# Filter loop of a hybrid layer: chunk buffers laid apart, banks read back one by one, loop transfers in parts of 128 KB behind the first half of a quarter's products

## The chip, the cores and the metric

One core of a Trainium2 chip. The metric is the device time of one execution in microseconds (us). The kernel before was run three times: 1398.19, 1403.44 and 1407.6 us, a median of 1403.44 us. One more execution was profiled.

## The reference, cut to what matters

The program takes `x`, 8 sequences of 1024 tokens with 128 channels, through two residual layers. Layer 0 is attention over normalised heads; layer 1 is a two-directional state-space block and then a spectral filter. The change lies wholly in the spectral filter and in the hand-over to it, so only that is shown:

```python
def _compute_spectral(u, sigma, phi, Mpp, Mpm):
    U_plus, U_minus = _stu_conv(phi, u, PADDED_SL)     # FFT convolution of u with 16 filters
    s = sigma ** SIGMA_POW
    out = jnp.einsum('btkd,k,kde->bte', U_plus, s, Mpp)
    return out + jnp.einsum('btkd,k,kde->bte', U_minus, s, Mpm)
...
t = t + _L1_ffn_ref(_ln_t(t), ...)                     # spectral filter + three-tap regression
```

The kernel does the convolution in the frequency domain: it transforms the normalised tokens to 128 frequencies, forms for each frequency a matrix (128 by 128, for several phases) out of the filters' spectra and the mixing matrices, multiplies, and transforms back.

## The kernel before, in words

Three stages of the program matter here. Engines run the instructions of each stage in the order in which they are written; in the first two groups below this holds for TensorE, VectorE, ScalarE and GpSimd (`IN_ORDER`), while the DMA issues of SyncE (SP) are placed by a planner.

**The preparing stage** (pools `f_1`, `f_2`, about 998 to 1069 us in the profile). A loop over sequences `b` = 2 to 8. `transform(b)` turns the tokens (`cpt`, L561), makes their spectra on TensorE (`pf`, L571), combines them on VectorE and GpSimd (`sd` L582, `sp` L586 and L589) and stores 1 MB of spectra to DRAM (`ud`, L592). `taps_of(b - 1, k)` makes the three-tap regression (`pu`, L601), `add_taps` adds it to the residual `X` (L611), and `store_residual` writes 512 KB of `X` to DRAM (`xa`, L614). In between, `turned(n)`, for b = 2 to 5, reads a quarter of the mixing bank, 512 KB (`md`, L1568), turns it on TensorE (`mdt`, L1573), copies it (`me`, L1574) and stores it (L1577). Only after the fourth bank are all four read back, in four transfers of 512 KB, into the tile `mst` (L1580), which the filter loop multiplies with. `reload(u)` (L1320), the last read-back of a residual, stands in the stage before it.

**The filter loop** (pools `g_2`, `g_3`). 16 chunks of 8 frequencies, software pipelined: iteration `c` makes the matrices of chunk `c + 1` and applies those of chunk `c`, in four quarters. A quarter is two calls of `matrices` (TensorE `pg`, L1644, four PSUM tiles each, copied out to `gs` by ScalarE, L1657, and VectorE, L1655, in turn) and two calls of `apply` (TensorE `py`, L1678), then `gather` (L1693 to L1699). The input spectra of a chunk come in two transfers of 256 KB (`u`, L1664), for which GpSimd then makes a second, rotated copy (L1667, L1668). Every second quarter stores 256 KB of sums (`yd`, L1701); `fetch` reads a part of an earlier chunk's sums back (`early_yt`, L1709). `gs` and `u` are double-buffered tiles of the pool `g_2`. That pool takes the memory which the residuals `X` held, so its first writers wait until the last `xa` store has read them.

**The last chunk and the inverse transform.** In the last iteration no matrices are made; instead 3 MB of residuals are asked for in two transfers (`load_residuals`, L1712). After it the sums are read back (L1753), transformed (`pz`, L1769), added to the residuals (L1776) and written out (L1779).

Of the kernel before, what the change touches and what calls it, by code (L numbers as in the profile page):

```python
# [14 lines left out]
P = 128  # L15
B = 8
# [29 lines left out]
def fast_kernel(ctx: ExitStack, tc: tile.TileContext, a: dict, out: bass.AP, bad: bass.AP):  # L46
# [883 lines left out]
    with ExitStack() as s:  # L930
# [611 lines left out]
        reload(u)  # L1542
# [10 lines left out]
    with ExitStack() as s:  # L1553
        mp = s.enter_context(tc.tile_pool(name="c_m", bufs=1, side="right"))
        mst = mp.tile([P, 32, C], F32, tag="mst", name="mst")
        early_yt = mp.tile([P, 2, 4, 4, C], F32, name="early_yt")

        with ExitStack() as s2:
            p1 = s2.enter_context(tc.tile_pool(name="f_1", bufs=1))
            p2 = s2.enter_context(tc.tile_pool(name="f_2", bufs=2))  # L1560
            ps_f = s2.enter_context(tc.tile_pool(name="f_ps_f", bufs=2, space=PSUM))
# [3 lines left out]
            def turned(n, pool, tag, size):  # L1565

                t = p2.tile([P, 8, C], F32, tag="md", name=f"md{n}")
                nc.sync.dma_start(t, md.rearrange("d r k e -> d (r k) e")[:, n * 8 : n * 8 + 8, :])  # L1568
                to = p2.tile([P, 8, C], F32, tag="me", name=f"me{n}")
                for at in range(0, 8, size):  # L1570
                    pt = pool.tile([P, size, C], F32, tag=tag, name=f"mdt{n}_{at}")
                    for i in range(size):
                        nc.tensor.transpose(pt[:, i, :], t[:, at + i, :], ident)  # L1573
                    nc.vector.tensor_copy(  # L1574
                        to[:, at : at + size].rearrange("p k d -> p (k d)"), pt.rearrange("p k d -> p (k d)")
                    )
                nc.sync.dma_start(me[:, n * 8 : n * 8 + 8, :], to)  # L1577
                if n == 3:
                    for g in range(4):
                        nc.sync.dma_start(  # L1580
                            mst[g * 32 : (g + 1) * 32],
                            me[g * 32 : (g + 1) * 32].rearrange("n k d -> k n d"),
                        )
# [23 lines left out]
            s2.enter_context(tc.manual_schedule(engines=IN_ORDER))  # L1607
            uts = {}
            for _ in scaled(3, *third, p2):
                pass  # L1610
            for b in range(2, B + 1):
                if b + 2 < B:
                    norms[b + 2] = normalize(p2, b + 2)
                if b < B:
                    transform(b)
                if 3 < b + 1 < B:
                    for _ in normalized(b + 1, p2, *norms.pop(b + 1), wide=p2):
                        pass
                if b > 2:
                    taps_of(b - 1, 0)  # L1620
                if 2 <= b <= 5:
                    turned(b - 2, *((ps_o, "o", 4) if b == 2 else (ps_t, "t", 8)))
                if b > 2:
                    taps_of(b - 1, 1)
                    store_residual(b - 1)
        middle.close()
        middle.close()

        with ExitStack() as s2:
            p2 = s2.enter_context(tc.tile_pool(name="g_2", bufs=2))  # L1630
            p3 = s2.enter_context(tc.tile_pool(name="g_3", bufs=3))
            ps_g = s2.enter_context(tc.tile_pool(name="g_ps_g", bufs=8, space=PSUM))

            turn = 0

            def matrices(c, n, gs):

                nonlocal turn
                pts = [ps_g.tile([P, 4, P], F32, tag="g", name=f"pg{c}_{n}_{g}") for g in range(4)]
                cols = slice(c * FC, (c + 1) * FC)  # L1640
                for e in range(4):
                    for g in range(4):
                        rows = slice(g * 32, (g + 1) * 32)
                        nc.tensor.matmul(  # L1644
                            pts[g][:, e, :],
                            lhsT=mst[rows, n * 4 + e, :],
                            rhs=taps[rows, cols].rearrange("p f q m i -> p (f q m i)"),
                            start=True,
                            stop=True,
                        )  # L1650
                for g, pt in enumerate(pts):
                    to = gs[:, :, n * 16 + g * 4 : n * 16 + g * 4 + 4]
                    frm = pt.rearrange("p e n -> p n e")
                    if turn % 2:
                        nc.vector.tensor_copy(to, frm)  # L1655
                    else:
                        nc.scalar.copy(to, frm)  # L1657
                    turn += 1

            def loaded_spectra(c):  # L1660

                u = p2.tile([P, 2, NB, B, 2, 4 * FC], F32, tag="u", name=f"u{c}")
                for k in range(NB):
                    nc.sync.dma_start(  # L1664
                        u[:, 0, k].rearrange("p b i f -> p b (i f)"), ud[c][:, :, k].rearrange("p b i q f -> p b (i q f)")
                    )
                nc.gpsimd.tensor_scalar(u[:, 1, :, :, 0, :], u[:, 0, :, :, 1, :], -1.0, None, ALU.mult)  # L1667
                nc.gpsimd.tensor_copy(u[:, 1, :, :, 1, :], u[:, 0, :, :, 0, :])  # L1668
                return u
# [50 lines left out]
            for c in range(-1, chunks):  # L1720
# [21 lines left out]
                if c > 0:  # L1742
                    fetch(c - 1)
# [847 lines left out]
```

## Time and profile before

| quantity | us |
|---|---|
| median of three runs | 1403.44 |
| profiled execution, its own time | 1403.45 |
| its span, first to last instruction | 1401.6 |
| preparing stage | about 998 to 1069 |
| first matrices to first application | 1069.2 to 1088.4 |
| filter loop, first application to that of the last chunk | 1088.4 to 1340.8 |
| last chunk | 1340.8 to 1356.4 |
| inverse transform and output | 1356.4 to 1401.6 |

All times below that are places on the axis are counted from the first instruction of the profiled execution. PE is TensorE's matmul, PEld its weight load, DVE VectorE, ACT ScalarE, POOL GpSimd, SPq the DMA issues of SyncE. A row of the windows view gives, for a stretch A:B, the length, then the busy time of PE, PEld, DVE, ACT and POOL with the number of instructions in brackets, then the share of full clock granted to TensorE (PEclk), the mean busy share of the 16 DMA engines and the rate in GB/s. A row of the waits view reads: who waited, for whom, the total in us, how often, and the longest. A row of the timeline gives start and length of a run of like instructions, and in brackets the idle time before it and what ended it; "issue" stands for a wait that the profile cannot put down to any engine or transfer.

### The profile page before, as it was taken

To read this page: it belongs to the slowest core of one execution; us is meant where nothing else is said; L and a number is where in the kernel's file an instruction comes from. 1 tells how busy PE (TensorE), PEld (TensorE's weight loads), DVE (VectorE), ACT (ScalarE), POOL (GpSimd) and SP (SyncE) were. 2 spreads that over 40 slices of the span, in tenths; PEclk is the share of its full clock that TensorE was granted. 3 is DMA by queue.
4 is the path that set the end of the run, shared out by engine and by line. 5 is a ranking of instruction groups with operands and counts; after the bars stand their busy time and mean duration, and the time that the engine had idled before them with its cause. 6 is when DMAs were issued, how large, how long until landed. Compare 5 with 4: busy or idle time off the path is not lost. (4 is left out here: it accounts for less than half of the span.)

```text
span 1401.6 us, 47569 instructions
## 1 busy us (share of the span) xinstructions
PE 1330.1 (95%) x20926; PEld 844.7 (60%) x20926; DVE 1103.4 (79%) x2145; ACT 922.8 (66%) x1428; POOL 536.0 (38%) x510
## 2 busy tenths in 40 slices
PE   7999999999999999999999999998898999999967
PEld 4333333333333666666666666667797988888964
DVE  5789888788778688988889898999564777777745
ACT  5666666766756888888878888876353555555520
POOL 3412986876910343434343343444673011111100
PEclk9999999999999999999999999999999999999979
DMA  7100111111101434444444343431668132222357
GB/s 172 55 2 2 38 39 39 53 39 39 31 1 42 96 78 93 108 94 113 94 108 94 92 95 88 114 83 48 197 208 198 46 78 73 77 69 70 83 171 294
DMA packets 139391, 123.24 MB, mean 88 GB/s; under 512 B 44808, under 2 KB 118152, under 8 KB 135080
## 3 DMA queue, kind: packets, MB, share of 16 engines
q1 hardware_dynamic: 137048, 115.93, 32.0%
q8 instruction: 166, 2.72, 0.8%
q10 hardware_dynamic: 2128, 4.19, 0.8%
q14 instruction: 49, 0.40, 0.1%
HBM read 78.15 MB, written 34.08 MB: 80 GB/s over the span
## 5 line engine op out<-in xcount | busy, mean ns | idle before, releaser
L809 ACT ACTIVATE pr<-pt 128x1024 f32<-128x1024 f32 x256 | 248.2, 1022 | 105.0 <-PE pt L804 103.9
L1657 ACT COPY gs<-pg 128x512 f32<-128x512 f32 x256 | 133.1, 603 | 75.6 <-PE pg L1644 58.4
L1655 DVE COPY gs<-pg 128x512 f32<-128x512 f32 x256 | 159.1, 685 | 26.0 <-PE pg L1644 18.9
L834 DVE TENSOR_TENSOR two<-pr,pr 128x1024 f32<-128x1024 f32 x128 | 164.8, 1328 | 15.2 <-ACT pr L809 15.2
L804 PE MATMUL pt<-q,k 32*128 32x512 f32 x1024 | 162.5, 651 | 6.1 <-ACT pr L809 4.1
L1644 PE MATMUL pg<-taps,mst 32*128 32x128 f32 x4096 | 150.1, 283 | 11.9 <-issue 5.8
L1644 PEld LDWEIGHTS pg<-taps,mst 32*128 32x128 f32 x4096 | 135.0, 189 | 27.2 <-issue 19.3
L825 PE MATMUL po<-pr,v 128*32 128x512 f32 x1024 | 140.6, 610 | 0.0
L1678 PE MATMUL py<-gs,u 128*32 128x128 f32 (+1 forms) x4096 | 130.9, 281 | 3.4 <-issue 3.4
L1030 POOL TENSOR_TENSOR ec<-ec,ct 128x2048 f32<-128x2048 f32 x16 | 83.6, 5224 | 112.3 <-ACT ct L1110 57.1
L1072 DVE SCALAR_TENSOR_TENSOR xs<-xp,cw,xs 128x1024 f32<-128x1024 f32 x96 | 122.5, 1283 | 2.2 <-issue 0.2
L1678 PEld LDWEIGHTS py<-gs,u 128*32 128x32 f32 (+1 forms) x4096 | 114.8, 141 | 10.9 <-issue 3.6
L1094 PE MATMUL pb<-bxt,wbc 128*128 128x512 f32 x256 | 114.0, 597 | 3.6 <-ACT zs L1085 3.6
L1667 POOL TENSOR_SCALAR u<-u 128x512 f32<-128x512 f32 x16 | 24.0, 1499 | 237.5 <-DMA u<-ud 138.3
L804 PEld LDWEIGHTS pt<-q,k 32*128 32x128 f32 x1024 | 49.5, 185 | 88.9 <-ACT pr L809 27.1
L1193 DVE SCALAR_TENSOR_TENSOR state<-state,dec,pst 128x64 f32<-128x64 f32 x448 | 87.3, 275 | 1.1
L1302 POOL TENSOR_TENSOR rms<-rms_v,mhalf 128x8 f32<-128x8 f32 x16 | 26.5, 1659 | 157.0 <-DVE rms_v L1300 157.0
L1094 PEld LDWEIGHTS pb<-bxt,wbc 128*128 128x128 f32 x256 | 47.1, 189 | 60.3 <-issue 55.0
L825 PEld LDWEIGHTS po<-pr,v 128*32 128x32 f32 x1024 | 27.8, 110 | 89.7 <-issue 86.4
L1016 POOL TENSOR_TENSOR lm<-cs,lm 128x2048 f32<-128x2048 f32 x16 | 57.9, 3620 | 57.7 <-DVE xs L1072 22.6
L845 PE MATMUL pd<-two,ones 128*32 128x512 f32 x512 | 74.1, 618 | 2.3 <-DVE two L834 2.1
L1272 PEld LDWEIGHTS spo<-wo,y 128*128 128x128 f32 x512 | 62.1, 191 | 13.1 <-issue 8.9
(310 smaller groups left out, 2784.5 us busy)
## 6 DMA issues: line engine op xcount, KB each, us to landing
lm<-cd SPq DMA_DIRECT2D x32, 512.0 KB
ec<-cd SPq DMA_DIRECT2D x32, 512.0 KB
ud<-sp SPq DMA_DIRECT2D x8, 1024.0 KB
u<-ud SPq DMA_DIRECT2D x32, 256.0 KB
yd<-sums SPq DMA_DIRECT2D x32, 256.0 KB
moved<-state SPq DMA_DIRECT2D x48, 128.0 KB
room<-yd SPq DMA_DIRECT2D x6, 1024.0 KB
X<-in_x SPq DMA_DIRECT2D x8, 512.0 KB
```

The source lines that it names most:

```text
L804: nc.tensor.matmul(pt[:, i, :], lhsT=k[rows, j * P : (j + 1) * P], rhs=q[rows, cols], start=True, stop=True)
L809: nc.scalar.activation(pr[:, 2 * g : 2 * g + 2, :].rearrange("p i t -> p (i t)"), pt.rearrange("p i t -> p (i t)"), AF.Exp, scale=SCALE,)
L825: nc.tensor.matmul(po[rows, :], lhsT=vs[b][:, j, rows], rhs=pr[:, h, :], start=(j == 0), stop=(j == NT - 1))
L834: nc.vector.tensor_tensor(two, sums["pr"][:, 2 * g : 2 * g + 2, :], pr[:, 2 * g : 2 * g + 2, :], ALU.add)
L1030: t = nc.gpsimd.tensor_tensor(u.ec, u.ec, u.ct.unsqueeze(1).to_broadcast([P, NH, NT, L]), ALU.mult)
L1072: u.convolved = nc.vector.scalar_tensor_tensor(acc, xp[:, at : at + T], cw[u.d][:, n, i : i + 1], acc, ALU.mult, ALU.add)
L1094: nc.tensor.matmul(u.pb[:, i * 512 : (i + 1) * 512], lhsT=wbc[u.d][:, k, :], rhs=xt[:, at : at + 512], start=(k == 0), stop=(k == KC - 1),)
L1193: nc.vector.scalar_tensor_tensor(u.state[:, k, h, :], u.state[:, k - 1, h, :], u.dec[:, c, h, j : j + 1], u.pst[c][:, j, h, :], ALU.mult, ...
L1644: nc.tensor.matmul(pts[g][:, e, :], lhsT=mst[rows, n * 4 + e, :], rhs=taps[rows, cols].rearrange("p f q m i -> p (f q m i)"), start=True, ...
L1655: nc.vector.tensor_copy(to, frm)
L1657: nc.scalar.copy(to, frm)
L1678: nc.tensor.matmul(py[t * 32 : t * 32 + 32 - 16 * m, q // 2, :], lhsT=u[:, i, m:, :, :, q * FC + f].rearrange("p k b i -> p (k b i)"), rhs ...
```

## The change

Six edits.

1. `gs` and `u` of even chunks live in a pool `c_g`, opened before the preparing stage on the other side of the memory; those of odd chunks in a pool `g_g` opened with the loop. Chunk 0's buffers thus no longer lie over the residuals. `early_yt` moves to a pool of its own that opens with the loop. The wide temporaries of the preparing stage get their own pool `f_x`.
2. Banks are loaded ahead (`load_bank`): three before the loop over `b`, the fourth when the first has been turned. `turned` moves from b = 2 to 5 to b = 3 to 6. `reload` of the last residual moves behind the first bank load.
3. Each bank is read back by itself (`spread(n)`, at the head of b = 4 to 7): sixteen transfers of 128 KB instead of four of 512 KB.
4. The first two of the eight `matrices` calls of chunk 0 are made inside the preparing stage, at b = 8, one between the last two tap blocks and one after them (`double_banks`, using the PSUM banks of the spectra). Chunk 0's spectra are asked for at the end of that stage.
5. In the loop every `u` comes in four parts of 128 KB with their own pair of GpSimd copies, every `yd` store in two halves, and the residuals in six transfers of 512 KB. Each of these, and `fetch`, is made to wait (`behind`) for the last matmul of the first of the two `apply` calls in a quarter; only the first half of each store follows the `gather` instead.
6. SP's DMA issues are in written order too, in both stages (`ALL_IN_ORDER`).

The numbers of matmuls, of evictions and of bytes are the same.

```diff
-        early_yt = mp.tile([P, 2, 4, 4, C], F32, name="early_yt")
+        first_gs = s.enter_context(tc.tile_pool(name="c_g", bufs=1, side="right"))
...
+        def load_part(u, c, part, other=None):
+            k, h = divmod(part, 2)
+            bs = slice(4 * h, 4 * h + 4)
+            t = nc.sync.dma_start(
+                u[:, 0, k, bs].rearrange("p b i f -> p b (i f)"), ud[c][:, bs, k].rearrange("p b i q f -> p b (i q f)")
+            )
+            if other:
+                behind(t, other)
+            nc.gpsimd.tensor_scalar(u[:, 1, k, bs, 0, :], u[:, 0, k, bs, 1, :], -1.0, None, ALU.mult)
+            nc.gpsimd.tensor_copy(u[:, 1, k, bs, 1, :], u[:, 0, k, bs, 0, :])
...
+            def spread(n):
+                for g in range(4):
+                    nc.sync.dma_start(
+                        mst[g * 32 + n * 8 : g * 32 + n * 8 + 8],
+                        me[g * 32 : (g + 1) * 32, n * 8 : n * 8 + 8].rearrange("n k d -> k n d"),
                     )
-                nc.sync.dma_start(me[:, n * 8 : n * 8 + 8, :], to)
-                if n == 3:
-                    for g in range(4):
-                        nc.sync.dma_start(
-                            mst[g * 32 : (g + 1) * 32],
-                            me[g * 32 : (g + 1) * 32].rearrange("n k d -> k n d"),
-                        )
...
-            s2.enter_context(tc.manual_schedule(engines=IN_ORDER))
+            s2.enter_context(tc.manual_schedule(engines=ALL_IN_ORDER))
+            for n in range(3):
+                load_bank(n)
+                if n == 0:
+                    reload(units[-1])
...
+            planned = {(B, 1): 1, (B, 2): 1}
             for b in range(2, B + 1):
+                if 4 <= b <= 7:
+                    spread(b - 4)
...
                 if b > 2:
                     taps_of(b - 1, 0)
-                if 2 <= b <= 5:
-                    turned(b - 2, *((ps_o, "o", 4) if b == 2 else (ps_t, "t", 8)))
+                ahead(b, 1)
+                if 3 <= b <= 6:
+                    turned(b - 3)
...
+            us = {0: loaded_spectra(0, first_gs)}
+            for part in range(4):
+                load_part(us[0], 0, part)
...
+            def amid_products(c, n, made):
+                if n == 0 and c > 0:
+                    store(c - 1, 1, 1, late_sums.pop((c - 1, 1)), made)
+                if n == 2:
+                    store(c, 0, 1, late_sums.pop((c, 0)), made)
+                if c + 1 < chunks:
+                    for part in ((0,), (1, 2), (3,), ())[n]:
+                        load_part(us[c + 1], c + 1, part, made)
+                if c > 0 and n >= 2:
+                    fetch(c - 1, n - 2, made)
+                if c + 1 == chunks:
+                    for _ in range(2 if n < 2 else 1):
+                        waiting.pop(0)(made)
...
-                        apply(c, half, turn, gs[c], us[c], py)
+                        made = apply(c, half, turn, gs[c], us[c], py)
+                        amid_products(c, n, made)
                         apply(c, half, turn + 2, gs[c], us[c], py)
                         gather(c, half, turn, py)
+                        behind_products(c, n)
```

## The prediction

> **What bounds the kernel now.** I read the page's first part, then a table of windows cut at the stage boundaries, then the waits and the timeline inside the bad windows.
>
> ```profile
> PE 1330.1 (95%) x20926; PEld 844.7 (60%) x20926; DVE 1103.4 (79%) x2145; ACT 922.8 (66%) x1428; POOL 536.0 (38%) x510
> ```
>
> TensorE is busy for 95% of the span, so a gain must come from places where it idles or runs below its clock. The windows view finds them (columns: PE, PEld, DVE, ACT, POOL, clock, DMA share, GB/s).
>
> ```profile
> 1003.00:1008.00 5.00, 0.00 (x1) 0.03 (x1) 1.39 (x3) 1.49 (x3) 5.00 (x11) 0.91 0.99 292
> 1008.00:1015.00 7.00, 7.00 (x27) 6.38 (x28) 3.48 (x18) 0.35 (x1) 3.37 (x7) 0.58 1.04 346
> 1015.00:1053.00 38.00, 38.00 (x293) 36.61 (x293) 24.31 (x62) 20.63 (x48) 27.31 (x53) 1.00 0.62 209
> 1069.00:1076.00 7.00, 2.07 (x64) 1.88 (x64) 0.25 (x2) 0.19 (x1) 0.00 (x0) 0.96 0.66 235
> 1076.00:1082.00 6.00, 5.55 (x93) 5.56 (x97) 4.99 (x8) 4.01 (x8) 0.89 (x1) 0.50 0.94 178
> 1088.40:1340.80 252.40, 246.52 (x7554) 224.71 (x7553) 184.84 (x413) 138.08 (x296) 28.83 (x28) 1.00 0.27 71
> 1340.80:1356.40 15.60, 12.11 (x321) 11.56 (x320) 4.34 (x15) 2.19 (x8) 0.00 (x0) 0.78 0.70 243
> ```
>
> Two stalls of 5 us, at 1003 and at 1071, are each followed by 6 to 7 us at about half clock; the loop has 6 us of idle matmul time; the last chunk idles and loses clock too. The waits between 995 and 1090 us name the first two stalls:
>
> ```profile
> ACT gs L1657 <- DMA xa<-X: 16.5, 1, 16.5
> PE mdt L1573 <- DMA md<-md: 5.1, 1, 5.1
> PE pg L1644 <- ACT gs L1657: 5.2, 1, 5.2
> ```
>
> The first turning waits for the load of bank 0; later the PSUM tiles fill because the first copies into `gs` wait for the last residual store. In the loop the timeline shows a quarter without and one with a stall:
>
> ```profile
> 1111.11 2.26 PE L1644 MATMUL pg<-taps,mst 32*128 32x128 f32 x64
> 1113.29 2.01 PE L1678 MATMUL py<-gs,u 128*32 128x128 f32 x64
> 1115.24 2.25 PE L1644 MATMUL pg<-taps,mst 32*128 32x128 f32 x64
> ...
> 1121.15 0.52 SPq L1664 DMA_DIRECT2D u<-ud  x1
> 1121.52 2.01 PE L1678 MATMUL py<-gs,u 128*32 128x128 f32 x64
> 1123.46 1.16 PE L1644 MATMUL pg<-taps,mst 32*128 32x128 f32 x29
> 1124.87 1.38 PE L1644 MATMUL pg<-taps,mst 32*128 32x128 f32 x35 [0.25 <-issue]
> ```
>
> A free quarter takes 1115.24 - 1111.11 = 4.13 us. The stalled one breaks in the middle of `pg` with no engine or transfer to wait for, 2 to 4 us after a `u` load. The last chunk has the same, longer:
>
> ```profile
> PE py L1678 <- issue: 3.4, 1, 3.4
> ```
>
> [...] queue q8, kind "instruction", 166 packets and 2.72 MB, 16 KB each. [...] the DMA records of the loop do show one about every 4.1 us. In free quarters around 1113 it starts as `py` starts (1113.32 against 1113.29) and takes 0.9 to 1.5 us; at 1122 it starts 0.73 us late, amid `u` packets. I read "issue" as a late fetch. [...] between 1338.73 and 1347.19 no fetch is recorded while residual packets fill the engines. [...]
>
> **The change part by part.** (a) Banks ahead. Bank 0 is now wanted at b = 3 and its load is issued where it was, at 1001, so the 5.1 us wait goes. What is late next: the second `transform` needs the PSUM tile that ScalarE copies out until 1004.5, so `cpt` of b = 3 starts at 1004.5 instead of 1009.7, a 1.6 us idle remaining. An undisturbed b with a turning takes 10.56 us (`cpt` at 1022.36 and 1032.92). Before, b = 7 began at 1053.17; after, 1004.5 + 4 x 10.56 = 1046.8. That includes the fourth turning, about 1 us, moved into b = 6. Gain 6.4 us: the wait, plus the half-clock tail.
>
> The DMAs moved on SP's ordered queue: bank 0's load now has the `xa` store of b = 1 and `reload` behind it; `reload` waits for its own store (2.3 us before) with two bank loads behind it, both wanted ten us and more later; each `spread` waits for the `me` store before it, and the next `ud` store stands behind that. Does `mst` come in time? The fourth bank is copied near 1045; its store stands behind the `ud` of b = 6, ready near 1047.6 (6.7 us behind its `pf`, as before). At 346 GB/s (window 1008 to 1015) that 1 MB, the 512 KB of `me` and the 512 KB of `xa` take some 6 us, and the last spread, 512 KB at the 180 GB/s seen while `mst` was read (1055 to 1061), 3 more: landing near 1057. From the head of b = 7 to the end of the taps it took 1069.22 - 1053.17 = 16.05 us; the first early `matrices` stands one tap block (2.7 us) before its end, at 1046.8 + 13.4 = 1060.2. So 3 us of slack; if everything runs at 180 GB/s, about 3 us are lost, and clock with them. I take 0.
>
> (b) Chunk 0 ahead, own memory. From the end of the taps to the first application it took 1088.4 - 1069.2 = 19.2 us. Now the first `gs` copies wait for nothing. Eight calls lie behind the taps (six of chunk 0, two of chunk 1), paced by VectorE: two copies of 0.685 us per call, 1.4 us, so 11.2 us, and 1.2 us at the start because the PSUM banks of the second early call must be emptied: 12.4. The early call inside the taps adds 1.05 us. Gain 19.2 - 13.4 = 5.8 us. The last two `xa` stores and chunk 0's `u` (1.5 MB, 4.5 us at 346 GB/s, behind `ud` of b = 7) and the GpSimd copies of `u`, with nothing queued behind them there, are hidden under these 12 us; with that cover gone they cost 0 to 3 us. (a) and (b): 12 us, 8 to 14.
>
> (c) Loop. 58 quarters lie between the `pg` runs at 1090.38 and 1338.64: 248.3 us against 58 x 4.12 = 239.0, so 9.3 us of stalls. A trigger halfway through `py` comes 1 us after the fetch began; packets follow an issue by 1 us, and 128 KB is half of the 1.5 us that a 256 KB load takes, so one or two parts lie between 2.0 and 3.7 us after `py`'s start, the next fetch at 4.1. The half store behind `gather` still meets the fetch, with half its bytes. But fetches late in the loop begin with `pg` (1309.95 against 1309.90), where parts now fall. Gain 0 to 9.3; a loss up to 3 if more parts mean more meetings; I take 7. The bill elsewhere: 8 GpSimd copies of 128 x 128 instead of 2 of 128 x 512 (1.50 and 0.61 us) per chunk. Bounds: 2.1 us if only elements count, 8.4 if a copy costs the same; I take 3, hidden either way beside a 16.5 us chunk. SP waits behind TensorE: the last part is issued 11.4 us into a chunk, and is wanted at 18.6; landing (3 us) and two copies leave about 3 us.
>
> (d) Last chunk. Four `apply` pairs of 1.95 us are 7.8; it takes 15.6. The same 3 MB in 512 KB pieces still fill 8 us at 390 GB/s, so a fetch can still be late, by one or two pieces instead of by 2 MB. Gain 0 to 7.8; I take 4. The extra store and its issue cost 0.3 us before the final read-back, whose 7.4 us stall stays.
>
> Sum: 12.2 + 7 + 4 - 0.3 = 22.9 us. The profiled execution took 1403.45 us (span 1401.6), the median is 1403.44, so the same sum serves: 1380.5.
>
> **The rivals.** One: only the hand-over gains, because the fetch drifts into the parts and the last chunk stays as it is: 1403.4 - 12 = 1391. For it: the phase late in the loop, and the unchanged bytes. Against it: two thirds of the quarters run free even now, and the long breaks follow a `u` load. Two: everything is recovered, 14 + 9.3 + 6 = 29: 1374. For it: free quarters are exactly periodic. Three, slower: SP's ordered queue makes the parts of `u` late. If the wake-up, landing and GpSimd copies of part 3 take over 7.2 us, TensorE stands at each chunk's first `apply`; at 3 us beyond that, 15 chunks cost 45 us: 1403.4 - 12 + 45 = 1436; it becomes slower overall from about 1 us per chunk. Against it: a `u` load before was followed by its GpSimd copy 5 us after the second issue (1121.15 to 1126.11), 256 KB and twice the copy. Four: `mst` late and clock lost again, hand-over gains 5, the loop nothing: 1398. That the transfers do not move is ruled out by the built order: SP's issues do wait on TensorE.
>
> **How the numbers follow.** Forecast (1376 to 1389) 0.56, rival two (1369 to 1376) 0.18, rival one (1389 to 1395) 0.13, rival four 0.06, rival three 0.07. The range 1369 to 1395 leaves out 0.13 by the cases and a little for a hand-over better than counted. One per cent, 14 us, is about what a measurement of this kernel can tell from no change: below 1389.4 is faster (0.75), up to 1417 the same (0.18), above it slower (0.07).
>
> **What would show it.** `cpt` of b = 7 near 1047; no wait of `mdt` for `md` nor of `gs` for `xa`; the first application near 1076 with full clock before it; quarters of 4.1 us with "issue" gaps under 3 us in all; the last chunk near 11 us. Wrong if `pg` waits for `mst`, if `py` waits for GpSimd's copies, or if the "issue" gaps are as many as before at other places.

## The result, and the profile after

The changed kernel takes 1416.64 us, the median of six runs (1416.10 to 1419.77), against 1401.54 us for the kernel before beside it: a ratio of 1.0109 with a 95% interval of 1.0083 to 1.0135. It is slower by about 1%; 1380.5 was forecast. The profiled execution took 1416.49 us with a span of 1414.7, so 13.0 us more than the one before (1403.45 and 1401.6). Cut at the same events in both traces, the 13.1 us of the spans are made up like this:

| stretch | before, us | after, us | difference | forecast |
|---|---|---|---|---|
| start to `cpt` of b = 0 | 962.24 | 963.13 | +0.9 | 0 |
| `cpt` of b = 0 to `cpt` of b = 7 | 90.93 | 84.60 | -6.3 | -6.4 |
| `cpt` of b = 7 to the first application | 35.26 | 58.98 | +23.7 | -5.8 |
| filter loop, to the last run of applications | 252.37 | 245.54 | -6.8 | -7.0 |
| last chunk, inverse transform, output | 60.84 | 62.42 | +1.6 | -3.7 |

Two rows are as forecast, one is 29.5 us off, one 5.3. The first part of the page of the changed kernel, busy time by engine:

```profile
PE 1325.0 (94%) x20926; PEld 841.1 (59%) x20926; DVE 1103.8 (78%) x2144; ACT 922.3 (65%) x1428; POOL 551.7 (39%) x606
```

The row of the filter's matrices in the page's table of groups (behind the second bar stands the idle time before the group, then what ended most of it):

```profile
L1594 PE MATMUL pg<-taps,mst 32*128 32x128 f32 x4096 | 149.2, 281 | 27.9 <-DMA mst<-me 24.7
```

TensorE does the same 20926 matmuls in 5 us less busy time, and idles more. One releaser owns the idle time: the read-back of the banks. The waits between 995 and 1110 us of the same trace:

```profile
ACT gs L1607 <- PE pg L1594: 43.3, 5, 35.2
PE pg L1594 <- DMA mst<-me: 24.7, 4, 20.1
POOL sp L586 <- DMA ud<-sp: 14.6, 2, 9.8
```

The waits that the prediction quoted, `mdt` for `md` (5.1 us), `pg` for `gs` (5.2) and `gs` for `xa` (16.5), are gone. In their place stands `pg` waiting for `mst`, four times. The timeline of TensorE shows the four as steps:

```profile
1080.36 0.79 PE L1594 MATMUL pg<-taps,mst 32*128 32x128 f32 x2 [20.11 <-DMA mst<-me]
1082.61 0.79 PE L1594 MATMUL pg<-taps,mst 32*128 32x128 f32 x2 [1.46 <-DMA mst<-me]
1085.46 0.79 PE L1594 MATMUL pg<-taps,mst 32*128 32x128 f32 x2 [2.06 <-DMA mst<-me]
1087.32 2.07 PE L1594 MATMUL pg<-taps,mst 32*128 32x128 f32 x26 [1.07 <-DMA mst<-me]
```

Two matmuls run whenever one more part of 128 KB has landed; the landing records of these four lie at 1079.7, 1082.4, 1084.8 and 1087.2 us. The parts come from four sets of four issues, and SP's timeline shows how the queue went:

```profile
1043.85 1.70 SPq L1635 DMA_DIRECT2D mst<-me  x4
1045.65 0.39 SPq L592 DMA_DIRECT2D ud<-sp  x1
1046.13 9.41 SPq L1631 DMA_DIRECT2D me<-me  x1
1059.85 1.50 SPq L1635 DMA_DIRECT2D mst<-me  x4
1061.93 8.92 SPq L1631 DMA_DIRECT2D me<-me  x1
1075.46 1.49 SPq L1635 DMA_DIRECT2D mst<-me  x4
```

One bank follows the other every 15.8 us, while TensorE comes round a `b` every 10.56. The issue of a `me` store lasts 9 us: the one begun at 1061.93 ends at 1070.85, when the four parts ahead of it are nearly through (their last landed at 1071.4). The next set reads what this store writes, so it waits until the store has landed (1075.4), and was issued at 1075.46, 28 us after the head of b = 7.

How slow a part is can be read from the transfers' answer for one stretch, whose row "GB/s" gives 40 equal slices of it. First the kernel before, 1055 to 1064 us, with parts of 512 KB to 32 partitions:

```profile
GB/s 177 177 175 171 175 177 180 173 175 168 178 187 193 221 225 193 184 191 175 180 180 175 171 198 234 155 171 168 162 162 166 168 180 175 166 182 189 241 303 344
```

Then the changed kernel, 1063 to 1072 us, with parts of 128 KB to 8 partitions (up to slice 13 the `ud` store runs beside them, from slice 33 on the `me` store):

```profile
GB/s 214 162 134 162 164 182 203 223 214 230 216 225 221 121 100 50 48 50 46 50 50 48 50 48 48 48 50 46 48 50 48 48 48 98 127 146 177 314 435 350
```

About 175 GB/s against 48. Two windows rows of the changed kernel (columns as in the table of the prediction) show what it costs TensorE: nothing runs, and the first figure behind the brackets, the granted clock, is half.

```profile
1067.00:1070.00 3.00, 0.00 (x0) 0.00 (x0) 0.00 (x0) 0.00 (x0) 0.00 (x0) 0.50 0.67 49
1082.00:1085.00 3.00, 0.79 (x2) 0.49 (x2) 0.00 (x0) 0.00 (x0) 0.00 (x0) 0.50 0.66 49
```

The loop and the end, in the same view:

```profile
1106.70:1352.20 245.50, 244.32 (x7553) 224.37 (x7552) 184.95 (x413) 137.78 (x295) 44.83 (x118) 1.00 0.33 74
1352.25:1362.20 9.95, 9.68 (x321) 8.94 (x320) 4.33 (x15) 2.14 (x7) 0.76 (x2) 1.00 0.62 176
1362.20:1369.50 7.30, 0.00 (x0) 0.00 (x0) 0.89 (x4) 0.27 (x1) 0.00 (x0) 0.76 1.04 276
1369.50:1376.80 7.30, 0.00 (x0) 0.00 (x0) 0.00 (x0) 0.00 (x0) 0.00 (x0) 0.50 0.49 123
```

In the loop TensorE idles for 1.2 us instead of 5.9. The last chunk's products take 9.95 us instead of 15.6, free of stalls; but then `pz` waits 14.7 us for the sums, where the waits of before had 7.6, and the end as a whole is no shorter. Where this wait comes from is seen in SP's issues. In the kernel before the last store of sums was issued 1.3 us after the last product (1357.57 against 1356.28); in the changed kernel the last two were issued 4.5 us after it (1366.66 against 1362.14), and the fetch of what they write at 1373.30, when they had landed. In the second half of the wait the transfers are busy for half the time only (0.49 in the last row): a chain of waits fills that half, not bytes.

### The profile page after: what moved, and what is told of

Its sections match the earlier page's. It is cut to its first block, busy times and chain, and to the rows that moved or that the text cites. A ratio compares the mean times of both kernels' runs of the same rounds, so it can differ in the third digit from the quotient of the medians.

```text
span 1414.7 us, 47838 instructions
## 1 busy us (share of the span) xinstructions
PE 1325.0 (94%) x20926; PEld 841.1 (59%) x20926; DVE 1103.8 (78%) x2144; ACT 922.3 (65%) x1428; POOL 551.7 (39%) x606
## 5 line engine op out<-in xcount | busy, mean ns | idle before, releaser
L1594 PE MATMUL pg<-taps,mst 32*128 32x128 f32 x4096 | 149.2, 281 | 27.9 <-DMA mst<-me 24.7
L1582 POOL TENSOR_SCALAR u<-u 128x128 f32<-128x128 f32 x64 | 34.0, 531 | 241.5 <-DMA u<-ud 203.3
L1026 ACT ACTIVATE lm<-lm 128x1024 f32<-128x1024 f32 x64 | 65.7, 1052 | 7.1 <-POOL lm L1016 6.9
```

Of the source, the lines that this page charges most:

```text
L1594: nc.tensor.matmul(pts[g][:, e, :], lhsT=mst[rows, n * 4 + e, :], rhs=taps[rows, cols].rearrange("p f q m i -> p (f q m i)"), start=True, ...
```

## The experiments

The theory was that the read-back in parts to 8 partitions is slow in itself and takes away the whole gain of the hand-over. Twelve runs, in three groups: what makes `mst` late, what the loop owes to what, and what the end is bound by. Each ratio is against the kernel before, measured beside it on the same chip. "b = 0 to 7" below is the stretch from the first `cpt` after 960 us to that of b = 7.

### Whole read-backs in the changed kernel

```diff
-                        mst[g * 32 + n * 8 : g * 32 + n * 8 + 8],
-                        me[g * 32 : (g + 1) * 32, n * 8 : n * 8 + 8].rearrange("n k d -> k n d"),
+                        mst[g * 32 : (g + 1) * 32],
+                        me[g * 32 : (g + 1) * 32].rearrange("n k d -> k n d"),
...
-                if 4 <= b <= 7:
+                if b == 7:
                     spread(b - 4)
```

> The changed kernel with one part undone: the four banks are read back together, in four transfers of 512 KB (32 partitions each), at the head of b = 7, everything else as changed. Theory A (a piece of 128 KB goes to 8 partitions, [...] takes 2.4 us, against 2.9 us for a piece of 512 KB, so sixteen pieces take 40 us instead of 12 and everything queued behind them is late): the four pieces land by about 1066, the first early matrices wait some 5 us instead of 27, the first application comes near 1085 instead of 1106.7, the time is 1390 to 1399. Theory B (SP's written order is the cause: a read-back that waits for its store holds up the stores behind it): the last store still stands behind the spectra of b = 6 in the written order, so the time stays over 1408.

1398.75 us, ratio 0.9988 (0.9966 to 1.0010). By the two ratios (1.0109 and 0.9988) the read-back bank by bank in parts cost the change some 17 us. This run alters two things at once, the shape of a transfer and the turns in which stores and read-backs follow each other; the two runs on the kernel before, further below, alter the shape alone. What is left of the wait, in the waits of this run's TensorE:

```profile
PE pg L1594 <- DMA mst<-me: 7.3, 4, 2.5
```

`mst` is still late, since the read-back starts at 1057.36, behind the last bank's store.

### Read-backs in pairs of banks

```diff
-                        mst[g * 32 + n * 8 : g * 32 + n * 8 + 8],
-                        me[g * 32 : (g + 1) * 32, n * 8 : n * 8 + 8].rearrange("n k d -> k n d"),
+                        mst[g * 32 + n * 16 : g * 32 + n * 16 + 16],
+                        me[g * 32 : (g + 1) * 32, n * 16 : n * 16 + 16].rearrange("n k d -> k n d"),
...
-                if 4 <= b <= 7:
-                    spread(b - 4)
+                if b in (5, 7):
+                    spread((b - 5) // 2)
```

> The changed kernel with two banks read back at a time: eight transfers of 256 KB to 16 partitions each, at the heads of b = 5 and b = 7. Theory A, with the number of engines as the cause: [...] a piece takes about 1.5 us, each pair 6 us; the last lands before 1061, the first early matrices do not wait, the first application comes near 1077, the time is 1383 to 1392. If instead the few partitions of a piece slow every packet (110 ns against 57), a piece takes 2 to 2.5 us, eight take 16 to 20 us and the time is 1390 to 1400. Theory B: over 1408, since the written order is kept.

1397.07 us, ratio 0.9989 (0.9964 to 1.0013). The landing records of the last four parts lie 2.3 to 2.7 us apart (1060.3, 1063.0, 1065.6, 1067.9), as far as those of parts of half the size. Each part now leaves sixteen landing records, where a part to 8 partitions leaves eight. The rate of the transfers, 1060 to 1068 us:

```profile
GB/s 92 100 97 90 97 100 87 92 108 95 100 115 138 105 102 97 90 97 92 97 100 95 97 97 95 95 95 90 100 97 92 92 102 90 95 138 212 259 340 343
```

The busy share of the 16 transfer engines is 0.9 or more in all 40 slices of this stretch, where it was 0.67 beside the parts to 8 partitions (1067 to 1070 us of the changed kernel). At that share the rate is 96 GB/s, twice that of the parts to 8 partitions and half of what 32 partitions had. So the number of engines at work cannot be the whole cause, and of the two outcomes that the expectation gave, the second came: a part takes 2.3 to 2.7 us. Of the wait for `mst` 6.6 us are left.

### The planner instead of the written order

```diff
-            s2.enter_context(tc.manual_schedule(engines=ALL_IN_ORDER))
+            s2.enter_context(tc.manual_schedule(engines=IN_ORDER))
```

(in the preparing stage alone)

> The changed kernel with SP's issues in the preparing stage placed by the planner again, as before; the sixteen pieces of 128 KB stay. Theory A: the pieces still take 40 us of the queue, the early matrices still wait more than 15 us, the time stays between 1408 and 1422. Theory B: the time falls to 1380 to 1395.

1416.58 us, ratio 1.011 (1.006 to 1.016), and nearly the same wait. The written order of SP's issues is not the cause.

```profile
PE pg L1594 <- DMA mst<-me: 24.0, 4, 19.6
```

Nor is it that SP is held while it issues the store:

```profile
1041.65 3.48 SPq L1635 DMA_DIRECT2D mst<-me  x4
1045.23 0.62 SPq L1631 DMA_DIRECT2D me<-me  x1
1056.63 3.27 SPq L1635 DMA_DIRECT2D mst<-me  x4
1060.00 0.85 SPq L1631 DMA_DIRECT2D me<-me  x1
1071.21 3.29 SPq L1635 DMA_DIRECT2D mst<-me  x4
```

Here the issue of the store takes 0.6 to 0.9 us, and yet the sets follow each other every 15.0 and 14.6 us. The store issued at 1045.23 lands at 1056.6, behind the four slow parts ahead of it, and only then can the next set go.

### Small parts in the kernel before

```diff
                     for g in range(4):
-                        nc.sync.dma_start(
-                            mst[g * 32 : (g + 1) * 32],
-                            me[g * 32 : (g + 1) * 32].rearrange("n k d -> k n d"),
-                        )
+                        for m in range(4):
+                            nc.sync.dma_start(
+                                mst[g * 32 + m * 8 : g * 32 + m * 8 + 8],
+                                me[g * 32 : (g + 1) * 32, m * 8 : m * 8 + 8].rearrange("n k d -> k n d"),
+                            )
```

> The kernel before with nothing changed but the read-back of the banks: at the same place sixteen transfers of 128 KB instead of four of 512 KB. The disputed cost by itself. Theory A: 16 x 2.45 = 39 us instead of 11.7, so the first matrices, which began at 1069.2, wait until about 1092 to 1097; the time is 1420 to 1432, 20 to 30 us over the kernel before. Theory B: within 5 us of the kernel before.

1412.28 us, ratio 1.0114 (1.0065 to 1.0164): this one edit makes the kernel before as slow as the whole change does. It is less than was expected. In the profile the first application came only 16.2 us later than before: the planner began the issues at 1044.4 instead of 1050.9. The loop of this profile was also 4.8 us shorter. The damage takes another way here, as the waits between 1040 and 1106 us show:

```profile
ACT gs L1658 <- DMA xa<-X: 35.4, 1, 35.4
PE pg L1645 <- DMA mst<-me: 13.1, 2, 7.6
```

Fourteen of the issues hold SP for 26.23 us, and the last residual stores, for which the copies into `gs` wait in this kernel, stand behind them.

### Parts of the same size to 32 partitions

```diff
-                    for g in range(4):
-                        nc.sync.dma_start(
-                            mst[g * 32 : (g + 1) * 32],
-                            me[g * 32 : (g + 1) * 32].rearrange("n k d -> k n d"),
-                        )
+                    for at in range(0, 32, 8):
+                        for g in range(4):
+                            nc.sync.dma_start(
+                                mst[g * 32 : (g + 1) * 32, at : at + 8],
+                                me[g * 32 + at : g * 32 + at + 8].rearrange("n k d -> k n d"),
+                            )
```

> The kernel before, with its four read-backs of 512 KB cut into sixteen of 128 KB the other way round: each part still goes to 32 partitions and takes a quarter of the rows of each (in the earlier run sixteen parts of the same size went to 8 partitions each, and that cost 14 us). Theory A (the time of a part follows the rows per destination partition, so few partitions make it slow): a part takes 0.7-1.2 us, all sixteen 12-19 us, and the time is within 4 us of the kernel before. Rival B (a transfer has a fixed time of some 2.5 us whatever its shape, so sixteen cost four times as much as four): time 10-16 us above the kernel before, as with parts of 8 partitions.

1398.66 us, ratio 0.9981 (0.9959 to 1.0003). Sixteen parts of 128 KB again, but their landing records are 0.65 us apart (1054.87, 1055.51, 1056.18, 1056.82 and so on). SP's timeline has all sixteen issues in 9 us:

```profile
1049.51 8.99 SPq L1581 DMA_DIRECT2D mst<-me  x16
```

The rate between 1055 and 1059 us is no lower than that of the whole read-backs:

```profile
GB/s 189 164 179 169 179 174 195 189 174 174 226 297 205 205 169 159 154 174 195 174 230 200 205 225 246 225 184 200 210 185 184 210 190 200 190 169 241 261 205 189
```

So it was neither the size nor the number of the transfers that mattered, but how they were cut. The four shapes side by side:

| part | destination partitions | rows of 512 B per partition | from landing to landing, us | rate, GB/s |
|---|---|---|---|---|
| 512 KB (before) | 32 | 32 | 2.7 to 2.9 | 175 |
| 256 KB (pairs) | 16 | 32 | 2.3 to 2.7 | 96 |
| 128 KB (changed) | 8 | 32 | 2.1 to 2.7 | 48 |
| 128 KB (wide) | 32 | 8 | 0.65 | 200 |

The time follows the rows per partition, 0.08 to 0.09 us each (2.5 / 32, 2.8 / 32 and 0.65 / 8), and hardly the number of partitions. In other words, the rate is nearly in proportion to the destination partitions of a transfer: about 6 GB/s for each (48 / 8, 96 / 16, 175 / 32 and 200 / 32). The records of single packets agree. Nearly all carry 512 B; one takes 0.11 us on average in the narrow parts (1067 to 1070 us) and 0.10 in the pairs (1062 to 1066), but 0.05 in both shapes with 32 partitions (1055 to 1060 before, 1055 to 1059 here).

One thing was not separated. The two fast shapes also read their source in one stretch (512 and 128 KB), the two slow ones in pieces of 8 and 4 KB.

### Banks early, read back whole

The question left is whether the rest of the hand-over was forecast rightly once `mst` is in time.

```diff
-                if 4 <= b <= 7:
-                    spread(b - 4)
+                if b == 6:
+                    for g in range(4):
+                        nc.sync.dma_start(
+                            mst[g * 32 : (g + 1) * 32],
+                            me[g * 32 : (g + 1) * 32].rearrange("n k d -> k n d"),
+                        )
...
-                if 3 <= b <= 6:
-                    turned(b - 3)
+                if 3 <= b <= 4:
+                    turned(2 * b - 6)
                 if b > 2:
                     taps_of(b - 1, 1)
                     store_residual(b - 1)
+                if 3 <= b <= 4:
+                    turned(2 * b - 5)
```

> The changed kernel with the four banks turned two at a time in b = 3 and b = 4, and read back in four transfers of 512 KB at the head of b = 6, so that mst can land before the first early matrices. Theory A (the hand-over of the change is sound, only mst was late): no wait of pg for mst, full clock, first application near 1077, time 1381-1390 us. Rival B (behind mst stands a second limit of about the same size, the copies into gs or the spectra of chunk 0): no wait for mst but first application still at 1085-1090, time 1392-1400.

1396.15 us over 20 runs (the profiled one 1392.59), ratio 0.9932 (0.9914 to 0.9950): faster than before, but 6 us slower than theory A had it and within the range of rival B. The first application, too, came at 1083.99 instead of near 1077. The stretches tell the two apart. No wait of `pg` for `mst` is left, and from `cpt` of b = 7 to the first application it took 30.27 us, where the prediction had 29.5 (35.26 less 5.8): there is no second limit behind `mst`, as rival B would have it. The loss lies earlier: b = 0 to 7 took 88.42 us instead of 84.60, and another 2.2 us against the profile of the changed kernel came before b = 0, where the two do not differ. The timeline of TensorE names the place:

```profile
1020.65 1.07 PE L561 MATMUL cpt<-ident,ln_x 128*128 128x128 f32 x8 [1.41 <-DVE me L1630]
1031.73 1.09 PE L1628 MATMUL mdt<-ident,md 128*128 128x128 f32 x8 [0.32 <-DVE me L1630]
1034.32 1.06 PE L561 MATMUL cpt<-ident,ln_x 128*128 128x128 f32 x8 [1.50 <-DVE me L1630]
```

Turnings and tokens share one PSUM tile; with two turnings in a `b` TensorE waits while it is emptied, 3.2 us in all.

### The fourth turning through another tile

```diff
-                if 3 <= b <= 6:
-                    turned(b - 3)
+                if 3 <= b <= 5:
+                    turned(b - 3, ps_t, "t")
                 if b > 2:
                     taps_of(b - 1, 1)
                     store_residual(b - 1)
+                if b == 5:
+                    turned(3, ps_f, "f")
```

(`turned` takes its PSUM pool and tag as arguments; the read-back is whole and at the head of b = 6, as above)

> The changed kernel with turnings at b = 3, 4 and 5, the fourth right behind the last taps of b = 5 through a PSUM tile of the spectra, and the banks read back in four transfers of 512 KB at the head of b = 6. Theory A (the 3.8 us that the run with two turnings at b = 3 and at b = 4 lost before b = 7 were waits for the one PSUM tile that turnings and tokens share): second to seventh turning of tokens in 84.5-86 us instead of 88.4, mst still in time, time 2-4 us below that run (1392-1394). Rival B (mst lands too late again, as it is issued 11 us before the head of b = 7): pg waits for mst 2-6 us and loses clock, time 1395-1402.

1388.76 us (1381.31 to 1391.31), ratio 0.9900 (0.9860 to 0.9940): this version is faster than both kernels, by more than was expected, and still well short of the 22.9 us that the prediction summed up. The stretch of the expectation, b = 0 to 7, took 84.62 us. The waits of TensorE between 995 and 1112 us are down to these:

```profile
PE pg L1594 <- DVE gs L1605: 2.0, 1, 2.0
PE cpt L561 <- ACT ut L566: 1.7, 1, 1.7
PE pf L571 <- DVE X L611: 0.7, 1, 0.7
PE pg L1594 <- DMA mst<-me: 0.7, 1, 0.7
```

`mst` was issued at 1044.27 and landed by 1058.1, 0.7 us late. With it in time, b = 0 to the first application took 84.62 + 31.22 = 115.84 us, against 126.19 before: a gain of 10.4 where the prediction summed 12.2.

### Unspaced transfers

```diff
         def behind(instruction, other):
-            tc.add_manual_dep(
-                ...
-            )
+            return
```

> Question: what gave the filter loop its 6.8 us. The changed kernel with `behind` doing nothing: parts of 128 KB, half stores, buffers and written order stay, but the transfers start as soon as SyncE reaches them. Theory A (they no longer fall on the instruction fetch because they wait for the first half of a quarter's products): the gaps with the mark issue come back, first application to last chunk's goes from 245.5 us to 250-253, time 1419-1426 us. Rival B (the smaller parts, the written order or the memory apart do it, the waiting does nothing): 245-247 us in the loop, time 1413-1418.

1419.67 us, ratio 1.0124 (1.0086 to 1.0163); 250.2 us in the loop, at the lower edge of theory A's range. The interval of the ratio overlaps that of the changed kernel.

### Two parts instead of four

```diff
-            k, h = divmod(part, 2)
-            bs = slice(4 * h, 4 * h + 4)
+            k, bs = part, slice(0, B)
...
-                    for part in ((0,), (1, 2), (3,), ())[n]:
+                    for part in ((0,), (1,), (), ())[n]:
```

> The changed kernel with each u in two transfers of 256 KB instead of four of 128 KB, still spaced behind the first half of a quarter's products (first and second quarter of a chunk). Theory A (the place counts, not the size): loop 245-247.5 us, time 1412-1418. Rival B (the size counts, 256 KB reach past the next instruction fetch): loop 249-253, time 1420-1426. Both leave the late banks as they are.

1421.86 us, ratio 1.0143 (1.0097 to 1.0189); 253.0 us in the loop. These are the numbers of rival B: this run speaks for the size of a transfer and not for its place alone.

### The kernel before once more

> The kernel before once more, for a second profile of its filter loop. Across profiles of kernels with one and the same changed loop, first application to the last run of applications took 244.2 to 249.5 us; the kernel before with small read-backs took 247.6, against 252.4 in its first profile. Theory A (the spacing takes out a real stall): again 251-253 us. Rival B (where the instruction fetch falls differs from run to run, and most of the 6.8 us was chance): 247-250 us.

254.19 us in the loop (the time 1403.49), above theory A's range and far from rival B's. The wait rows of TensorE in the loop, one fence per kernel: before again, two parts, unspaced, changed.

```profile
PE pg L1644 <- issue: 6.2, 17, 0.8
```

```profile
PE pg L1593 <- issue: 4.0, 12, 0.8
```

```profile
PE pg L1589 <- issue: 2.8, 10, 0.5
```

```profile
PE pg L1594 <- issue: 1.1, 4, 0.4
```

A single profile is not safe here. Eight profiles with one and the same changed loop (the changed kernel and the runs that alter only what lies around it) lie at 244.2 to 249.5 us, mean 246.9; four with the loop of before at 252.4, 254.2, 255.6 and, in the run with small parts, 247.6, mean 252.4. The difference of the means is 5.5 us, with a standard error of about 1.9 (from the two spreads). So the loop very likely gained, and "issue" waits went with it. Two parts (253.0) lie outside the range of the changed loop, unspaced ones (250.2) just outside. That both the small size and the spacing are needed is likely by these two; one profile of each does not settle it.

What an "issue" wait is can be read from the transfer records of all fourteen profiles. Their loops have 121 stops of TensorE of more than 0.15 us, nearly all of them marked "issue". After each of them TensorE goes on 1.25 to 1.62 us after the end of an instruction fetch (queue q8), whether that fetch took 0.9 us or 1.8. And a loop is longer the more of these stops it has: 0.7 us of them in 244.2 us (pairs), 3.5 in 250.2 (unspaced), 7.0 in 255.5 (wide parts). So the prediction's reading of "issue" as a wait for the instruction fetch is borne out; what made a fetch late is not shown by it.

### Residuals later, 2 MB of them

```diff
-                    for _ in range(2 if n < 2 else 1):
+                    if n < 2:
                         waiting.pop(0)(made)
...
             for i in range(2):
                 fetch(chunks - 1, i)
+            for load in waiting[:2]:
+                load(None)
...
                 if n == 2:
+                    for load in waiting[2:]:
+                        load(None)
                     load_residuals(0, 4, 4)
```

(on the version with two turnings in b = 3 and in b = 4)

> The same, and of the residuals only two transfers of 512 KB (those of the first output piece) are asked for inside the last chunk; two more stand behind the last fetch of sums, two behind the read-back of the other sums. Theory A (the 14.7 us for which pz waits for the sums are the last stores and the fetch standing behind 3 MB of residuals): that wait falls to 5-8 us, time 5-9 us below the kernel with early banks alone. Rival B (the residuals are needed at once, and are now what comes last): pz waits less, but the additions behind it wait for the residuals, and the time is within 2 us of that kernel.

1398.64 us (ratio 0.9980, 0.9955 to 1.0005), against 1396.15 without it. The wait of `pz` for the sums fell to 7.7 us, and more came back behind it: of the waits from 1340 us on,

```profile
PE pz L1864 <- SPq L2656: 9.2, 2, 5.7
PE pz L1864 <- DMA early_yt<-yd: 7.7, 1, 7.7
```

From the first `pz` to the end it took 48.6 us instead of 37.3. In the windows of this run the share of the transfers stands at 1.03 to 1.06 from 1350 to 1378. The loss is more than rival B's 2 us.

### Residuals later, 1 MB

```diff
-                    for _ in range(2 if n < 2 else 1):
+                    for _ in range(2 if n < 2 else 0):
                         waiting.pop(0)(made)
...
                 if n == 2:
+                    for load in waiting:
+                        load(None)
                     load_residuals(0, 4, 4)
```

(on the version with the fourth turning apart)

> The same, with the residual transfers of the third and fourth quarter of the last chunk (512 KB each) moved behind the last fetch of sums and into the read-back. Theory A (the end has room for 1 MB, 2.6 us at 400 GB/s, since the share of the transfers falls below 0.9 there): pz waits 3-6 us less for the sums and nothing waits later, time 2-5 us below the run without it. Rival B (the end is bound by bytes: what is moved comes back as a wait for residuals or sums, as when 2 MB were moved): within 2 us of it or slower.

1389.85 us (ratio 0.9923, 0.9898 to 0.9948), against 1388.76 without it. `pz` waited 9.8 us for the sums instead of 13.5, the last run of applications to the first `pz` shrank from 24.8 to 20.8, and the first `pz` to the end grew from 38.1 to 43.1. This is rival B, and the run before goes the same way: bytes moved behind the fetch are paid at the end.

## Why the prediction was wrong

**The failed step is in part (a): "Does `mst` come in time?"** It ended "landing near 1057", with 3 us of slack, "I take 0". The last part landed near 1087. Two numbers in that step were wrong. First, the price of a spread, "512 KB at the 180 GB/s seen while `mst` was read (1055 to 1061), 3 more". That rate belongs to parts that go to 32 partitions. The four parts of a bank, to 8 each, ran at 48 GB/s, and took some 10 us. The step divided bytes by a rate without asking whether the new shape keeps the rate; the wide parts show that the small size is not to blame (128 KB to 32 partitions ran at 200 GB/s), and the pairs that 16 partitions lie between. Second, what followed from it: the store of the next bank stands behind these parts among the transfers, and the next spread waits for that store. So the cycle of spread and store (15.8 us) is longer than a `b` (10.56), and the lateness adds up over the banks. The working had named this chain ("each `spread` waits for the `me` store before it") but gave it no price of its own. It cost 24.7 us of waiting, and half the clock with it (granted 0.50 from 1067 to 1070 and from 1082 to 1085 us). The early `matrices` inside the taps very likely made this worse (no run was made without them): they stand in TensorE's order ahead of the last tap block (`pu` at 1089.33), so that this too stood still.

**The rest of (a) and (b) held.** The wait for `md` went, and b = 0 to 7 became 6.3 us shorter where 6.4 were forecast; this stretch took 84.5 to 84.9 us in every profile of the changed order, but for the two runs with two turnings in a `b` through one tile. With whole read-backs and `mst` 0.7 us late, b = 0 to the first application gained 10.4 us of 12.2. Of the missing 1.8, 0.7 is that lateness, and 0.8 the stop of 2.0 us behind `DVE gs`, for which the working had 1.2.

**(c) held in its sum; its mechanism is open in part.** 7 were forecast, 6.8 came in the profile, 5.5 in the mean of several; that the first two agree so closely is luck, since profiles of one and the same loop differ by 5 us. The "issue" waits shrank as the working said (5.8 to 1.1 us). That the place behind the first half of `py` does it is not shown: two parts of 256 KB, issued in such places too, gained nothing.

**(d) failed in two terms.** A saving in the chunk was rightly forecast, from a wrong sum: "Four `apply` pairs of 1.95 us are 7.8" left out one. The row quoted has 321 matmuls, so five runs of 64, 9.75 us; the free part of 15.6 was 5.9, and in this profile the change got all of it (9.95) instead of "4". Part of that is luck, too: in the three other profiles with the last chunk of before it took 13.6 to 13.8 us, and in the five others with the changed one 10.0 to 11.6, some 3 us less. The term that failed is "the final read-back, whose 7.4 us stall stays". It became 14.7: the last stores and the fetch behind them now came after the residuals. The growth of this one wait, 7.1 us, is the whole of what the end lost again (5.65 saved in the chunk, 1.6 lost in all). The other profiles agree: this wait was 6.9 to 7.6 us with the order of before and 12.1 to 14.7 with that of the change. In the two runs with later residuals the bytes moved past that wait came back as later ones.

**The rivals.** Rival four, "`mst` late and clock lost again", had the right cause with the wrong size: it let the hand-over keep 5 us of its 12, where the hand-over became 17.4 us slower (-6.3 and +23.7), and it was given a chance of only 0.06. Rival three, the one above the time before, did not come: `py` waited 0.2 us for GpSimd's copies. The first sign under "Wrong if", "`pg` waits for `mst`", is what the trace shows.

**The engines.** A part to 8 partitions left eight landing records and ran at 48 GB/s, with the transfers' busy share at 0.67. The low share cannot be the whole loss, since pairs of banks, with sixteen records a part and a share of 0.9 or more, were still at 96 GB/s; and as the rate is in proportion to the partitions in all four shapes (about 6 GB/s for each), no run shows what the number of engines costs by itself.

## What to carry to other kernels

When a transfer is cut into smaller ones, ask along which axis: cut so that every part still goes to as many partitions, with fewer rows of each, and price a new shape by a transfer of that shape, not by its bytes: here parts of 128 KB ran at 48 GB/s to 8 partitions and at 200 to 32. This was not open to a read-back bank by bank in transfers like these: a bank holds 8 of the 32 partitions of each group, so early parts are narrow ones. The version with the fourth turning apart got `mst` nearly in time by turning all banks earlier and reading them back whole. When producer, store and read-back share one ordered queue, compare the time of their cycle with that of the engine's loop (15.8 against 10.56 us here), since a cycle that is longer is late by more with each turn. And a stall that has been removed can come back as a longer wait further on, as the 5.65 us saved in the last chunk did in the 7.1 us by which the wait for the sums grew; so follow the transfers, their order and their bytes, up to the end of the program before counting it as a gain.

## What was unexpected of the hardware

- A transfer of rows of 512 B took about 0.08 us per row and destination partition, hardly depending on how many partitions it had, so that the rate grew with the partitions, by about 6 GB/s for each (48 GB/s to 8, 96 to 16, 175 to 200 to 32). What the limit is (the destination partitions, or the way in which the source is walked) was not tried.
- The busy share of the transfers says little of their rate: at 49 GB/s it stood at 0.67 (changed kernel, 1067 to 1070 us), at 409 GB/s at 1.05 (kernel before, 1379 to 1382 us).
- Each of the 121 stops of TensorE of more than 0.15 us in the loops of fourteen profiles ended 1.25 to 1.62 us after the end of an instruction fetch (queue q8), whether the fetch took 0.9 us or 1.8.
- The same loop with the same instructions took 244.2 to 249.5 us in eight profiles. This spread of 5.3 us is as large as the gain argued over.
